# Six instead of seven chunks with a head block taken ahead, two steps sooner, and a tail shared between two engines

## The chip, the cores and the metric

The kernel runs on one NeuronCore of a Trainium2 chip. The core has a matrix engine (PE, with its weight loads as PEld), a vector engine (DVE), a scalar engine (ACT), a general engine (POOL) and a queue engine for DMAs (SP). Each works through its own list of instructions in order; they meet only where one waits for another's result. The metric is the device time of one execution in microseconds (us): the median of the kernel before is 1092.4 us over 3 runs (1090.79 to 1093.73).

## The reference, cut to what matters

Two layers of a transformer on x of shape (16, 256, 128), all in fp32, each with adaptive layer norms: attention and a mixture of 16 experts in the first layer, a "holographic" attention and a channel mix in the second. The change touches only the second layer and how its work is spread over the first layer's experts.

```python
h = _layernorm(x) * (1 + ca) + sa                 # layer 1, first half
k_real = (h @ Wk).reshape(Bb, Tt, H, D)           # H * D = 1024 columns
v = (h @ Wv).reshape(Bb, Tt, H, D)
k = jnp.exp(1j * (k_real * PHASE_SCALE))
rotors = jnp.exp(1j * (t[:, None, None] * freqs))[None]
# _holo_fused_step: real(cumsum(v * binder, over t) * probe) / sqrt(t + 1)
out_pos = _holo_fused_step(v, rotors, jnp.conj(rotors))
k_shifted = jnp.roll(k, 1, axis=1).at[:, 0].set(0.0)
out_assoc = _holo_fused_step(v, jnp.conj(k_shifted), k)
x = x + ga * ((out_pos * g_pos + out_assoc * g_assoc) @ Wo)
h = _layernorm(x) * (1 + cb) + sb                 # layer 1, second half
xr = mu_r * h + (1 - mu_r) * h_prev               # h_prev: h one time step back
xk = mu_k * h + (1 - mu_k) * h_prev
x = x + gb * sigmoid(xr @ W_r.T) * (square(relu(xk @ W_k.T)) @ W_v.T)
```

## The kernel before

The 16 batches are worked on in 8 chunks (`NCH`) of two batches. Tokens lie 128 to a partition block; transposed activations are `128 x 512` tiles (128 channels by two batches of 256 time steps). The program has three stages that follow one another, and a tail.

**Attention** (layer 0) goes over the 64 rounds of batches and heads.

**Experts** (from line 743): one step `n` per chunk `c` and expert `e`, so 128 steps, and 4 more to drain. A step projects gate and up on PE (L764, L766), forms `g` on DVE (L768), `u` on ACT (L770) and Silu on ACT (L773), clips `u` on POOL (L774), multiplies on DVE (L780) and on POOL by the routing weight (L781), and three steps later PE adds the down projection to `acc` (L789). At `e` 2 to 4 of the next chunk the finished chunk goes back into `x`; at `e == 5` DVE takes the figures (means and variances) of the next layer norm and at `e == 7` POOL turns them into a scale and an offset (`normalizer`). PE, DVE, ACT and POOL follow the program's order by hand (`manual_schedule`).

Beside the experts the layer-1 holographic work starts early. Its 1024 columns are 8 blocks of 128 (`NJ`). For the chunks below `AHEAD` (7 of 8) the last block, `j = 7`, is done during the experts of the chunk after, by the generator `part_ahead` (L885). One segment of it runs in each step: `tokens` (layer norm on ACT, L200), two steps later the transposes (L212) and the modulation (L218), then `v` (L899), then the phases `k` (L927), their offset (L944) and sine and cosine (L945 to L950), and then eight pieces (position and association, two batches, sine and cosine). A piece is a product on POOL (`bind`, L905), a running sum on DVE (L911), a product on DVE (L913) and a sum into `total` on DVE (L918). It starts at `e == 10`. For the last of the seven (`soon`, chunk 6, in the experts of chunk 7, which are the last) everything is drawn together: figures at `e == 4`, normalizer at `e == 5`, start at `e == 6`, transposes one step after the tokens, and its pieces are read in six steps. The part of chunk 5 still runs at that time, so two parts end with the experts.

**Holographic stage** (from line 1127): one step `n` per chunk and block, `PARTS[c]` blocks for a chunk: 7 for chunks 0 to 6 and 8 for chunk 7, 57 steps in all. A step is, on PE: keys and values of step `n + 2` (L1158, L1162) and the output projections (L1209, four 512-column matmuls, each seen as two instructions); on DVE: two running sums of 1024 columns (L1195), the phase offset (L1174) and one product (L1426); on POOL: two products for step `n + 1` (L1192) and one for step `n - 1` (L1431); on ACT: two copies out of PSUM (L1159, L1163) and three activations (L1180 to L1182). At block 3 of a chunk with a part ahead, one matmul adds `totals[c]` times `w_last` (L1218). For a chunk from `AHEAD` on, `tokens`, transposes and modulation happen in the chunk before it (L1470, L1475, L1409).

The channel mix of the chunk before runs beside it in places counted from that chunk's end (`place`): output at 0, into `x` at 1, means 2, variances 3, spread 4, norm 5, tokens 6, `pk2` and its squares 7, `pr2` 8, sigmoid and values 9, products 10 and 11, results 12 and 13. What is left for chunk 6 after place 7, and all of chunk 7, is the tail: `last_half` is a generator of six segments, one per batch of chunk 7, and the loop at L1494 goes through both halves segment by segment with the rest of chunk 6 in between. All layer-norm and gating products of both halves are on ACT there (L1358, L1364, L1384).

Tiles of the last stage lie in memory that the expert stage gives back, so their first writers wait for the last readers of what lay there.

## Time and profile before

| what | us | where it is from |
|---|---|---|
| median of the runs (3) | 1092.4 | times |
| the profiled execution's own time | 1093.5 | times |
| its span, first to last instruction | 1091.7 | page |
| attention | 0 to 303.6 | first L764 at 303.6 in the trace |
| experts | 303.6 to 689.4 | ACT takes the last `acc` (L798) at 689.44 |
| of these, experts of chunks 3 and 4 | 45.9 and 45.5 | L764 starts |
| of these, chunk 7 | 631.03 to 689.4 | L764 starts; L798 |
| first product of the next stage on DVE (L1426) | 692.83 | timeline |
| steady chunk of the holographic stage (7 steps) | 46.9 | L1426 starts |
| its last PE result read by ACT (L1227) | 1073.57 | timeline |
| tail, to the last result in `x` | 1088.4 | timeline |
| end of the span (last DMA) | 1091.7 | page |

The time around the span (1093.5 - 1091.7 = 1.8 us) is not changed by anything here. An engine row in a timeline reads: start, duration, engine, line, operation, output<-input, shape, count, and in brackets how long the engine stood idle before it and whose result ended that. Busy times in the page are sums of durations; consecutive instructions on one engine overlap a little, so the distance from one start to the next (0.33 us for a 128x256 DVE instruction whose row says 0.42) is what counts in a dense row.

### The profile page before, as it was taken

The page shows a single profiled execution, that of the slowest core. Times are in us where ns is not written, and L with a number is a line of the kernel's source. Part 1 is how long each engine was busy: PE and PEld are TensorE (multiplying, and loading weights), DVE is VectorE, ACT ScalarE, POOL GpSimd, SP SyncE. Part 2 cuts the span into 40 slices and gives each one's busy share as a digit, 9 for nine tenths or more (in the row PEclk, how much of TensorE's full clock was granted, in tenths as well). Part 3 has the DMA queues.
Part 4 walks back from the last instruction along what each step waited for, and adds up shares of the span by engine and source line. Part 5 has one row for each costly group of instructions (what it writes and reads, how often), then busy time and mean ns, then how long its engine had stood idle before and what let it go on. Part 6 is the DMA issues. An engine that isn't in the chain of part 4 may idle for free.

```text
span 1091.7 us, 16048 instructions
## 1 busy us (share of the span) xinstructions
PE 1025.6 (94%) x5319; PEld 519.0 (48%) x5319; DVE 910.8 (83%) x1417; ACT 687.6 (63%) x1391; POOL 803.1 (74%) x762
## 2 busy tenths in 40 slices
PE   7999999999999999999999999698999999999987
PEld 5566766666654444444444444233344443434333
DVE  6679878998766888887776778998999999999994
ACT  3676766667656476677756555364766766667573
POOL 2245334542658678788876988799999999999992
PEclk8999999999999999999999999799999999999999
DMA  4102100000042222222322221000000000000000
GB/s 115 42 10 69 52 4 3 2 4 3 22 174 82 94 90 86 96 98 78 98 93 81 84 92 58 1 0 0 1 0 10 5 6 10 1 10 1 10 6 24
DMA packets 31955, 46.80 MB, mean 43 GB/s; under 512 B 8032, under 2 KB 22784, under 8 KB 31872
## 3 DMA queue, kind: packets, MB, share of 16 engines
q1 hardware_dynamic: 31328, 45.51, 13.0%
q8 instruction: 42, 0.69, 0.3%
q14 instruction: 41, 0.34, 0.1%
q10 hardware_dynamic: 544, 0.26, 0.1%
HBM read 43.13 MB, written 2.37 MB: 42 GB/s over the span
## 4 chain that ended last, share of the span: by engine, by line
PE 55%; DVE 23%; ACT 8%; POOL 7%; issue 5%; DMA 1%; SPq 0%; DVEq 0%; ACTq 0%; POOLq 0%
PE pg L764 7%; PE acc L789 7%; PE pup L766 7%; DVE mem L1195 6%; DVE sum_assoc L1195 5%; PE s L404 5%; PE st L438 5%; PE po L458 5%; PE pout L1209 5%; DVE m_pos L1426 3%; POOL u L781 2%; PE pq L531 2%; DVE maxima L416 1%; PE pk L1158 1%; PE pk L539 1%
## 5 line engine op out<-in xcount | busy, mean ns | idle before, releaser
L446 ACT ACTIVATE exp<-st 128x512 f32<-128x512 f32 x256 | 132.2, 602 | 87.1 <-PE st L438 87.1
L416 DVE TENSOR_REDUCE maxima<-s 128x2 f32<-128x512 f32 x256 | 158.9, 684 | 26.6 <-PE s L404 26.4
L781 POOL TENSOR_TENSOR u<-u,wide 128x512 f32<-128x512 f32 x128 | 164.0, 1281 | 19.3 <-DVE u L780 10.1
L770 ACT ACTIVATE u<-pup,b_gu 128x512 f32<-128x512 f32 x128 | 87.5, 684 | 102.4 <-PE pup L766 86.4
L768 DVE TENSOR_SCALAR g<-pg,b_gu 128x512 f32<-128x512 f32 x128 | 95.6, 747 | 64.0 <-PE pg L764 63.2
L1209 PE MATMUL pout<-m_pos,w_pos 128*128 128x512 f32 x228 | 115.6, 631 | 31.2 <-DVE m_pos L1426 21.6
L789 PE MATMUL acc<-u,w_dn 128*128 128x512 f32 x256 | 134.3, 606 | 5.9 <-POOL u L781 5.8
L764 PE MATMUL pg<-hT,w_gu 128*128 128x512 f32 x256 | 132.0, 597 | 1.4 <-DVE u L780 0.9
L1195 DVE TENSOR_TENSOR_SCAN sum_assoc<-keep,bound_assoc 128x1024 f32<-128x1024 bf16 x57 | 130.0, 2280 | 1.2 <-POOL bound_assoc L1192 1.2
L766 PE MATMUL pup<-hT,w_gu 128*128 128x512 f32 x256 | 130.7, 592 | 0.0
L1195 DVE TENSOR_TENSOR_SCAN mem<-keep,bound_pos 128x1024 f32<-128x1024 bf16 x57 | 129.6, 2273 | 0.0
L1192 POOL TENSOR_TENSOR bound_assoc<-v,phasor 128x1024 f32<-128x1024 f32 x56 | 122.2, 2183 | 4.8 <-ACT phasor L1182 4.8
L1431 POOL TENSOR_TENSOR sum_assoc<-sum_assoc,phasor 128x1024 f32<-128x1024 f32 x57 | 124.5, 2185 | 0.7 <-DVE sum_assoc L1195 0.7
L1192 POOL TENSOR_TENSOR bound_pos<-v,rotor 128x1024 f32<-128x1024 f32 x56 | 122.3, 2185 | 2.8 <-DVE sums L911 2.8
L774 POOL TENSOR_SCALAR u<-u 128x512 f32<-128x512 f32 x128 | 81.0, 633 | 58.4 <-ACT u L770 51.8
L1209 PE MATMUL pout<-sum_assoc,w_assoc 128*128 128x512 f32 x228 | 107.3, 593 | 0.0
L780 DVE SCALAR_TENSOR_TENSOR u<-u,pg 128x512 f32<-128x512 f32 x128 | 86.9, 679 | 16.9 <-POOL u L774 12.7
L773 ACT ACTIVATE pg<-g 128x512 f32<-128x512 f32 x128 | 76.2, 595 | 27.5 <-DVE g L768 27.2
L1209 PEld LDWEIGHTS pout<-m_pos,w_pos 128*128 128x128 f32 x228 | 40.9, 194 | 101.4 <-DVE m_pos L1426 50.8
L1159 ACT ACTIVATE whole<-pk 128x512 f32<-128x512 f32 x55 | 32.8, 596 | 88.4 <-PE pk L1158 86.0
L438 PE MATMUL st<-qx,kx 32*128 32x256 f32 x1024 | 82.3, 389 | 1.1 <-DMA qx<-turned 1.0
L404 PE MATMUL s<-kx,qx 32*128 32x256 f32 x1024 | 78.2, 409 | 4.2 <-DVE kx L541 1.8
(301 smaller groups left out, 1850.6 us busy)
## 6 DMA issues: line engine op xcount, KB each, us to landing
wide<-scores SPq DMA_DIRECT2D x64, 512.0 KB
qx<-turned SPq DMA_DIRECT2D x256, 1.0 KB
w_gu<-in_gate_up_dram SPq DMA_DIRECT2D x8, 256.0 KB
out_dram<-x SPq DMA_DIRECT2D x16, 128.0 KB
x<-in_x_dram SPq DMA_DIRECT2D x14, 128.0 KB
w_dn<-in_down_dram SPq DMA_DIRECT2D x4, 256.0 KB
ga<-ga_rows SPq DMA_DIRECT2D x1, 768.0 KB
w_k<-in_Wk_dram SPq DMA_DIRECT2D x1, 512.0 KB
```

The lines of the kernel that those rows point to most:

```text
L404: nc.tensor.matmul(s[g][:, i, :], qs[c][r][rows_, k, ts(i, P)], ks[c][rows_, r // NS, k, :], start=True, stop=True,)
L416: nc.vector.tensor_reduce(mx[:, :, g], s[g], AX.X, ALU.max, negate=True)
L438: nc.tensor.matmul(st[g][:, i, :], ks[c][rows_, r // NS, k, ts(i, P)], qs[c][r][rows_, k, :], start=True, stop=True,)
L446: nc.scalar.activation(e[:, g, :, :], st[g], AF.Exp, scale=QSCALE)
L764: nc.tensor.matmul(pg, w_gu[:, e, 0 : 2 * D : 2], h2, start=True, stop=True)
L766: nc.tensor.matmul(pu, w_gu[:, e, 1 : 2 * D : 2], h2, start=True, stop=True)
L781: nc.gpsimd.tensor_tensor(u, u, wide[n // SOME][:, n % SOME, :], ALU.mult)
L789: nc.tensor.matmul(accs[c], w_dn[:, e, :], work.pop(n), start=False, stop=(e == NE - 1))
L1192: nc.gpsimd.tensor_tensor(w[nm], v2, bind, ALU.mult)
L1195: nc.vector.tensor_tensor_scan(dst.rearrange("p s k t -> p (s k t)"), keep.rearrange("p s t -> p (s t)"), work[n][nm].rearrange("p s k t - ...
L1209: nc.tensor.matmul(pos[c], w[:, j, :], m[:, k, :, :].rearrange("p k t -> p (k t)"), start=(j == 0 and i == 0 and k == 0), stop=(j == PARTS ...
L1431: nc.gpsimd.tensor_tensor(m, m, phasor[(n - 1) % 3][:, :, :, 1:], ALU.mult)
```

## The change

`AHEAD` goes from 7 to 6. So chunk 6 keeps all 8 blocks in the holographic stage (58 steps instead of 57), its part ahead with the compressed order (`soon`) is gone, and its tokens, transposes and modulation move into chunk 5's holographic steps. The six parts that remain start at `e == 8` instead of 10.

```diff
-AHEAD = NCH - 1
+AHEAD = NCH - 2
...
-                soon = c == AHEAD - 1
                 tokens(c)
                 yield
-                if not soon:
-                    yield
+                yield
...
-                if soon:
-                    for binds, reads in (((3,), (1,)), ((4,), (2,)), ((5,), (3,)), ((6,), (4,)), ((7,), (5,)), ((), (6, 7))):
-                        go(binds, reads)
-                        yield
-                    return
...
-                    if i and c < AHEAD - 2:
+                    if i:
                         added(pieces[i - 1][1])
...
-                if e == (4 if soon else 5) and c:
+                if e == 5 and c:
                     mv = figures(c - 1, "a1")
-                if e == (5 if soon else 7) and c:
+                if e == 7 and c:
                     figs[c - 1] = normalizer(c - 1, mv, fp, "a1")
...
-                if e == (6 if soon else 10) and 1 <= c <= AHEAD:
+                if e == 8 and 1 <= c <= AHEAD:
                     ahead.append(part_ahead(c - 1))
```

The last output projections go batch by batch, and `pk2` with its squares for chunk 6 leaves the last step for the tail:

```diff
-                out_project(n - 1, 1, w_assoc, m)
-                if n == last + 1:
-                    out_project(last, 0, w_pos, m_pos)
-            if 7 in place:
+                if n <= last:
+                    out_project(n - 1, 1, w_assoc, m)
+                else:
+                    for k in range(2):
+                        for i, (w, read) in enumerate(((w_assoc, m), (w_pos, m_pos))):
+                            for half in range(2):
+                                nc.tensor.matmul(
+                                    pos[NCH - 1][:, ts(k, T)],
+                                    w[:, NJ - 1, :],
+                                    read[:, half, k, :],
+                                    start=False,
+                                    stop=(k == 1 and i == 1 and half == 1),
+                                )
...
+            if 7 in place and n < last:
                 mixed(place[7], wk_now, wk_before, "pk2")
```

In the tail, `last_half` has seven segments. The four POOL instructions for scale and offset become two on DVE (add the epsilon; offset by one `scalar_tensor_tensor`) and one on POOL (the power). The norm of half 0 stays on ACT and that of half 1 goes to DVE; the modulation goes the other way round. The sigmoid's last step goes from ACT to DVE (`tensor_scalar`, add 1, times the gate), for both halves and for chunk 6.

```diff
+            nc.vector.tensor_scalar(rstd, mv[:, :, 1], EPS, None, ALU.add)
+            nc.gpsimd.tensor_tensor(rstd, rstd, neg_half, ALU.pow)
...
+            nc.vector.scalar_tensor_tensor(off, mv[:, :, 0], -1.0, rstd, ALU.mult, ALU.mult)
...
+                if k:
+                    nc.vector.tensor_scalar(
+                        hn[:, i, :], x[b][:, i, :], rstd[:, i : i + 1], off[:, i : i + 1], ALU.mult, ALU.add
+                    )
+                else:
+                    nc.scalar.activation(
+                        hn[:, i, :], x[b][:, i, :], AF.Identity, bias=off[:, i : i + 1], scale=rstd[:, i : i + 1]
+                    )
...
+            if k:
+                nc.scalar.activation(hz[:, 1:], tokens_, AF.Identity, bias=shift, scale=scale)
+            else:
+                nc.vector.tensor_scalar(hz[:, 1:], tokens_, scale, shift, ALU.mult, ALU.add)
...
-            nc.scalar.activation(r, r, AF.Identity, bias=gbT1[:, b : b + 1], scale=gbT1[:, b : b + 1])
+            nc.vector.tensor_scalar(r, r, 1.0, gbT1[:, b : b + 1], ALU.add, ALU.mult)
...
+        both_halves()
+        mixed(gone, wk_now, wk_before, "pk2")
+        mix_squares(gone)
+        mixed(gone, wr_now, wr_before, "pr2", left[:, 0])
+        r = hp.tile([P, 2, T], F32, tag="r", name=f"r_{gone}")
+        nc.scalar.activation(r, mix[gone], AF.Tanh, scale=0.5)
+        mix[gone, "r"] = r
+        mix_values(gone, left[:, 1])
+        both_halves()
+        both_halves()
+        for k in range(2):
+            nc.vector.tensor_scalar(r[:, k, :], r[:, k, :], 1.0, gbT1[:, 2 * gone + k : 2 * gone + k + 1], ALU.add, ALU.mult)
+            mix_gated(gone, k)
+        both_halves()
+        py = with_tokens_first(gone, mix.pop((gone, "r")), "py2", (p_out, "out"))
+        both_halves()
+        for k in range(2):
+            mix_out(2 * gone + k, py[:, k])
+        both_halves()
+        both_halves()
```

## The prediction

> **What bounds the kernel now.** I read the page's chain first, then busy time by stretches, then the timelines of the stretches where a bound changes hands.
>
> ```profile
> PE 55%; DVE 23%; ACT 8%; POOL 7%; issue 5%; DMA 1%; SPq 0%; DVEq 0%; ACTq 0%; POOLq 0%
> 631.00:664.00 33.00, 32.10 (x79) 14.16 (x78) 23.73 (x47) 18.71 (x35) 27.45 (x35) 1.00 0.28 96
> 664.00:694.00 30.00, 20.33 (x43) 7.79 (x41) 29.09 (x52) 10.85 (x19) 21.07 (x28) 0.88 0.05 18
> 694.00:1073.60 379.60, 347.76 (x838) 149.42 (x838) 362.20 (x280) 241.07 (x512) 369.05 (x185) 0.99 0.02 5
> ```
>
> The columns after a stretch are its length and the busy time of PE, PEld, DVE, ACT and POOL, then the granted clock. The experts are PE's (32.1 of 33.0), but their last 30 us are not: DVE is busy for 29.1 and PE for 20.3. Later POOL (97%) and DVE (95%) are both full. The timelines of that gap, PE, POOL and DVE:
>
> ```profile
> 654.21 1.49 PE L212 MATMUL pln_a<-ident,hn_a 128*128 128x128 f32 x4 [0.72 <-ACT hn_a L200]
> 676.38 1.13 PE L764 MATMUL pg<-hT,w_gu 128*128 128x512 f32 x2 [0.94 <-DVE u L780]
> 685.14 1.12 PE L789 MATMUL acc<-u,w_dn 128*128 128x512 f32 x2 [1.73 <-POOL u L781]
> 687.33 2.08 PE L789 MATMUL acc<-u,w_dn 128*128 128x512 f32 x2 [1.06 <-POOL u L781]
> ...
> 692.48 2.17 POOL L1192 TENSOR_TENSOR bound_pos<-v,rotor 128x1024 f32<-128x1024 f32 x1 [2.78 <-DVE sums L911]
> 694.61 2.17 POOL L1192 TENSOR_TENSOR bound_assoc<-v,phasor 128x1024 f32<-128x1024 f32 x1
> 696.75 2.18 POOL L1431 TENSOR_TENSOR sum_assoc<-sum_assoc,phasor 128x1024 f32<-128x1024 f32 x1
> ...
> 690.64 0.49 DVE L913 SCALAR_TENSOR_TENSOR sums<-sums,gates,phasor_ahead 128x256 f32<-128x256 f32 x1
> 691.17 0.42 DVE L918 TENSOR_TENSOR total<-sums,total 128x256 f32<-128x256 f32 x1
> 691.70 0.70 DVE L911 TENSOR_TENSOR_SCAN sums<-sums,und_ahead_assoc 128x256 f32<-128x256 f32 x1
> ```
>
> PE's last gate projection starts at 676.38 and its last `acc` only at 687.33. DVE is still summing pieces of the parts ahead at 691.70, and POOL's first product of the next stage waits 2.78 us for exactly that. From 692.48 POOL runs without a gap, 2.13 us from start to start, and the chain of waits goes through it to 736. So the next stage's clock starts at POOL's 692.48.
>
> **Part 1, the hand-over: -14.1 us.** Without the part of chunk 6, the stretch before 694 loses eight pieces on DVE: sum, product and addition, from start to start 0.73 + 0.53 + 0.34 = 1.60, so 12.8, and one offset (L944, 0.68). 29.1 busy of 30 becomes about 16: DVE no longer holds anything. PE loses `v` and `k` (two matmuls of 0.86), the transposes (0.44) and waits. Chunk 7's steps, from the L764 starts, were 2.57, but 4.26 at `e` = 3, 4.78 at 7, 3.44 and 3.43 at 8 and 9, and 3.68 at 14; without them 2.21 + 0.87 + 0.86 + 1.11 = 5.05 go, and the last gate projection starts at 676.38 - 5.05 = 671.33. What follows it I take from a quiet step, 522.53 in chunk 4: `g` ends 1.8 later, ACT's `u` and Silu at 3.2, POOL's clip at 3.6, DVE's product at 4.4, POOL's product at 5.7, and PE's `acc` needs 0.9 more: 678.0, where ACT could take `acc` only at 689.44 (half the clock then: 0.88 on average over the stretch). POOL's two small memsets (they waited for PE's `acc` in the trace too) take 0.3, so POOL starts at about 678.4 instead of 692.48: -14.1. The remaining part, of chunk 5, ends its last sum in step 127, before DVE's last expert product, so the 2.78 us wait has nothing left to wait for. DVE's first running sum then starts at about 676 and the second is done by 682; POOL needs it at 678.4 + 2 x 2.13 = 682.7. Bounds: -16, and -7.9 if the drain stays as long as it was (rival 1).
>
> **Part 2, two steps sooner: -1.5 us.** The parts of chunks 1 to 4 find steady PE-bound steps, and the same instructions merely change places: `v` and `k` at `e` 11 and 12 instead of 13 and 14. New is that `tokens` now follow `normalizer` by one step. In chunk 4 POOL ends its normalizer at 515.96 and ACT would be free for the tokens at 515.4: ACT waits 0.6 and is through at 517.65, its next `u` (516.78) comes 0.9 late, but POOL's clip of it started only at 518.70 and PE reads the tokens two steps later, at 520. Cost nothing; the cover is POOL's queue, and rival 2 is what it costs without it. One collision goes. In chunk 2's step `e` = 3 (6.73 us against 4.26 in chunk 3) ACT runs the router's exponential between the sines of part 0:
>
> ```profile
> 398.25 1.28 ACT L283 ACT_TABLE_LOAD   x1
> ...
> 400.04 1.28 ACT L950 ACT_TABLE_LOAD   x1
> ...
> 402.64 1.28 ACT L773 ACT_TABLE_LOAD   x1
> ```
>
> Two steps sooner the sine (L950) is before the exponential, and one of three loads goes (1.28). I take -1.5 with a little of the half clock that followed (407.2 to 410.6 at 0.50); bounds -3 and +2, the latter if the tokens at `e` = 8 of chunk 1 delay a DVE that is full with routing there.
>
> **Part 3, one step more: +6.75 us.** A step on the dense stretch takes POOL 3 x 2.13 = 6.40 and DVE 2.20 + 2.19 + 0.60 + 1.13 = 6.1. The L1426 starts give 6.10 to 6.43 for plain steps and 7.12, 7.30, 6.78 for the first three of a chunk. The work after chunk 6 spreads over one step more: `pk2` (1.72 on PE) falls in step 7 of chunk 6, `pr2` in the first of chunk 7. I put 7.0, 7.0, 7.3, three times 6.43, 5.96, 6.05 = 52.6 where the last chunk had 46.07: +6.5. Moving chunk 6's tokens and modulation into chunk 5 costs what chunk 7's cost in chunk 6, 6.68 instead of 6.43 in one step: +0.25. The dropped `w_last` matmul (0.86 on PE) is hidden. Bounds 6.1 and 7.6.
>
> **Part 4, the tail: -1.0 us.** Without `pk2` in the last step, PE's last projections start when POOL's product is ready (1069.25 instead of 1069.93) but then wait for DVE's (1070.5): they end 0.3 sooner. From there, counted from ACT's first `oT` (1073.57), before:
>
> ```profile
> 1076.66 0.60 ACT L1309 ACTIVATE r<-left 128x512 f32<-128x512 f32 x1 [2.25 <-PE left L1258]
> 1077.29 1.09 ACT L1312 ACTIVATE r<-r,gbT 128x256 f32<-128x256 f32 x2
> 1078.28 0.86 ACT L1358 ACTIVATE hn_last<-x,off_last,rstd_last 128x128 f32<-128x128 f32 x2
> ...
> 1080.51 0.87 ACT L1358 ACTIVATE hn_last<-x,off_last,rstd_last 128x128 f32<-128x128 f32 x2
> ```
>
> and the last result at 1088.43, 14.86 after. Now PE does `pk2` and `pr2` of chunk 6 first (1.72 each, 1.17 to 4.6); ACT's squares and tanh end at 5.25, so half 0's norm on ACT ends at 6.1 (5.6 before), while half 1's on DVE is ready at about 5.6 (7.8 before). Transposes to 6.6; modulation on DVE to 6.9, on ACT to 7.2 (8.8 before). Then PE in order: two `pk` 0.86 each to 8.6, chunk 6's transposes to 9.05, two `pr` to 10.75; tanh 11.2, DVE's scaling 11.55, chunk 6's two results 12.2, two products 12.95, transposes 13.2, last result 13.9: -0.95. I give 0.25 back for four output DMAs where two were. A DVE `tensor_scalar` of 128x256 in SBUF is not in the trace; I price it at 0.33 to 0.42 like other 128x256 rows (L1323), the tiny ones at 0.06 (a 128x4 memset) to 0.28 (reciprocal of 128x20), taking 0.2. Bounds of the part: -2.5 and +1.0.
>
> The Trainium skill, "VectorE: DVE Perf Modes", section "Mode 2×_2P", lets an fp32 `tensor_scalar` with source and result in SBUF run two elements a cycle; L849 (128x512 in SBUF, 0.77 us) shows no such halving. By the page the four scalings would save some 0.15 each, an estimate of 0.6 and a tail of -1.6.
>
> **Sum.** -14.1 - 1.5 + 6.75 - 1.0 = -9.85 on the span, 1091.7 to 1081.85. The profiled execution's own time is 1093.5, its surroundings stay at 1.8, so 1083.65 for that execution; against the median of 1092.4, which lies 1.1 below it, **1082.5**. About 0.3% (3.3 us) is what a measurement of this kernel can tell from no change.
>
> **Rivals.** 1, *the drain stays long*. The part of chunk 5 still sums until step 127, and if it or memory handed over holds DVE and POOL as now, the 13 us from last gate projection to finished `acc` (676.38 to 689.4) remain and the hand-over gives 5.05 + 2.8 = 7.9: 1082.5 + 6.2 = 1088.7. For it: ACT waits 2.28 there for nothing that the profile shows. Against it: DVE's load halves.
>
> 2, *the tokens stall PE in each of six chunks*, the slower side. Where the tokens follow one step after the normalizer today, in chunk 7, ACT waited 1.9 for POOL and PE stood (the L212 row). With a half-clock piece after it such a stall cost 2.47 in chunk 2. Six of them, 14.8, give 1097.3; from 1.64 a chunk the whole gain is gone. Against it: PE now reads the tokens two steps later.
>
> 3, *the half clock of 745.1 to 748.5 goes as well*. There PE waited 3.74 for `oT`; the distance between L1426 starts is 9.10, against 7.30 in later chunks. The pause is 3.74 long and may miss the window that decides: -1.8, 1080.7. Beside it, the Trainium skill ("TensorE: Matmul & The Clock Gate", "What's actually happening") has the clock set by free-running windows of about 3.4 us; the 3.4 us pieces agree.
>
> 4, *the parts cancel*: the step costs 7.6, the tail +1.0, and rival 1 holds: -7.9 - 1.5 + 7.6 + 1.0 = -0.8, 1091.6.
>
> **Chances.** Forecast 0.68, own range 1078.5 to 1087; rival 1 0.13, rival 2 0.06, rival 3 0.08, rival 4 0.05. Faster takes the forecast, rival 3 and two thirds of rival 1: 0.85; the rest of rival 1 and rival 4: 0.09; slower 0.06. Range 1077.5 to 1089.5: it leaves out rivals 2 and 4 and the ends of the others.
>
> **What would show it.** Part 1: POOL's first L1192 within 7 to 8 us of the last L764, no wait on L911. Part 2: two table loads around L283, chunk 2 at 46 to 47, no idle PE before L212. Part 3: 52 to 53 us from the L1426 start of chunk 6's eighth step to the last one. Part 4: last result 13 to 14.5 after `oT`. Wrong would be a late POOL start, or expert chunks over 46.5 throughout.

## The result, and the profile after

The changed kernel takes 1081.49 us, the median of 6 runs (1079.34 to 1084.76), beside 1091.79 us for the kernel before in 6 runs of the same chip. The ratio is 0.9905, with a 95% interval of 0.9892 to 0.9919: about 1% faster, 10.3 us. The profiled execution took 1081.84 us with a span of 1080.1 us.

First the page's chain of waits, by engine, and then busy time by stretches of the kernel after: length, then the busy time of PE, PEld, DVE, ACT and POOL with their instructions, then the granted clock, the share of the DMA engines and GB/s.

```profile
PE 59%; DVE 23%; ACT 6%; POOL 6%; issue 4%; DMA 1%; SPq 0%; DVEq 0%; ACTq 0%; POOLq 0%
```

```profile
628.00:658.00 30.00, 30.00 (x73) 13.25 (x72) 23.63 (x47) 13.73 (x25) 26.43 (x34) 1.00 0.26 92
658.00:676.00 18.00, 16.74 (x39) 7.11 (x38) 15.32 (x25) 7.03 (x13) 15.29 (x20) 1.00 0.14 53
676.00:1061.90 385.90, 351.75 (x860) 151.50 (x858) 368.90 (x283) 247.33 (x525) 376.70 (x188) 0.99 0.02 5
```

The last chunk of the experts is PE's throughout: 30.0 of 30, and 16.7 of the last 18, drain included. Before, PE had 20.3 of the last 30. The share of PE in the chain rises from 55% to 59%, that of ACT and POOL falls. In the long stage POOL stays full (376.7 of 385.9) and DVE nearly so (368.9); it is one step longer.

Now the hand-over of the kernel after, as timelines of PE, POOL and DVE. In this kernel the lines have moved: L1172 are the running sums (before L1195), L1169 the two products on POOL (L1192), L1413 the third (L1431), L1408 DVE's product (L1426), L1186 the output projections (L1209), L1204 `oT` (L1227); of a piece, L903 is the product, L909 the sum, L911 the product and L916 the addition.

```profile
668.50 1.02 PE L764 MATMUL pg<-hT,w_gu 128*128 128x512 f32 x2
673.26 2.35 PE L789 MATMUL acc<-u,w_dn 128*128 128x512 f32 x4 [1.17 <-POOL u L781]
...
671.94 2.49 POOL L781 TENSOR_TENSOR u<-u,wide 128x512 f32<-128x512 f32 x2
675.73 0.10 POOL L1021 MEMSET phasor<- 128x4 f32 x1 [1.30 <-PE acc L789]
675.86 2.18 POOL L1169 TENSOR_TENSOR bound_pos<-v,rotor 128x1024 f32<-128x1024 f32 x1
...
670.82 0.42 DVE L916 TENSOR_TENSOR total<-sums,total 128x256 f32<-128x256 f32 x1
673.42 2.30 DVE L1172 TENSOR_TENSOR_SCAN mem<-keep,bound_pos 128x1024 f32<-128x1024 bf16 x1
```

From the last gate projection to POOL's first product of the next stage it is 675.86 - 668.50 = 7.36 us (7.37 from the unrounded times), where it was 16.1. No sum of a part ahead stands there any more: the last addition starts at 670.82, and what POOL waits for is PE's `acc`.

The same points in both traces divide the gain. "S" is the start of POOL's first product of the next stage.

| us | before | after | difference | forecast |
|---|---|---|---|---|
| first gate projection of the experts | 303.62 | 303.41 | -0.2 | - |
| chunk 2 of the experts | 48.50 | 46.54 | -1.96 | -1.5 for chunk 2 and all |
| chunk 6 of the experts | 48.10 | 47.31 | -0.79 | 0 |
| the other chunks up to chunk 7's first projection | | | -0.1 | 0 |
| chunk 7's first projection to its last | 45.36 | 40.50 | -4.86 | -5.05 |
| drain, last projection to S | 16.09 | 7.37 | -8.72 | -9.05 |
| S to the last product on DVE (L1426, now L1408) | 376.78 | 381.82 | +5.04 | +6.75 |
| from there to ACT's first `oT` | 4.31 | 4.18 | -0.13 | -0.3 |
| `oT` to the end of the span | 18.15 | 18.20 | +0.05 | -0.7 |

They add up to -11.7, the difference of the two spans within rounding (1091.7 - 1080.1 = 11.6). One more thing matters below: the start of the experts itself varies from 300.9 to 303.6 us between the profiled executions, in kernels that are equal up to there, so experiments are compared by **the span less the first gate projection**, 788.1 before and 776.7 after, beside their medians.

### The profile page after: what moved, and what is told of

Same layout as the page of the kernel before. It is cut to its first block, busy times and chain, and to the rows that moved or that the text cites. A ratio compares the mean times of both kernels' runs of the same rounds, so it can differ in the third digit from the quotient of the medians.

```text
span 1080.1 us, 16033 instructions
## 1 busy us (share of the span) xinstructions
PE 1023.5 (95%) x5333; PEld 519.6 (48%) x5333; DVE 909.9 (84%) x1409; ACT 682.3 (63%) x1383; POOL 803.1 (74%) x750
## 4 chain that ended last, share of the span: by engine, by line
PE 59%; DVE 23%; ACT 6%; POOL 6%; issue 4%; DMA 1%; SPq 0%; DVEq 0%; ACTq 0%; POOLq 0%
PE pg L764 9%; PE acc L789 9%; PE pup L766 9%; DVE sum_assoc L1172 7%; DVE mem L1172 6%; PE s L404 5%; PE st L438 5%; PE po L458 5%; DVE m_pos L1408 4%; PE pout L1186 3%; PE pq L531 2%; DVE maxima L416 1%; POOL bound_pos L1169 1%; POOL u L781 1%; PE pk L539 1%
## 5 line engine op out<-in xcount | busy, mean ns | idle before, releaser
L781 POOL TENSOR_TENSOR u<-u,wide 128x512 f32<-128x512 f32 x128 | 163.9, 1281 | 16.1 <-DVE u L780 6.3
L1186 PE MATMUL pout<-m_pos,w_pos 128*128 128x512 f32 x228 | 114.7, 627 | 32.1 <-DVE m_pos L1408 23.2
L768 DVE TENSOR_SCALAR g<-pg,b_gu 128x512 f32<-128x512 f32 x128 | 95.6, 747 | 58.2 <-PE pg L764 56.9
L1172 DVE TENSOR_TENSOR_SCAN sum_assoc<-keep,bound_assoc 128x1024 f32<-128x1024 bf16 x58 | 132.3, 2282 | 1.8 <-POOL bound_assoc L1169 1.7
L1172 DVE TENSOR_TENSOR_SCAN mem<-keep,bound_pos 128x1024 f32<-128x1024 bf16 x58 | 131.9, 2274 | 0.0
L1169 POOL TENSOR_TENSOR bound_assoc<-v,phasor 128x1024 f32<-128x1024 f32 x57 | 124.3, 2181 | 3.9 <-ACT phasor L1159 3.9
L1413 POOL TENSOR_TENSOR sum_assoc<-sum_assoc,phasor 128x1024 f32<-128x1024 f32 x58 | 126.6, 2183 | 0.4 <-DVE sum_assoc L1172 0.4
L1169 POOL TENSOR_TENSOR bound_pos<-v,rotor 128x1024 f32<-128x1024 f32 x57 | 124.4, 2182 | 0.0
L1186 PE MATMUL pout<-sum_assoc,w_assoc 128*128 128x512 f32 x228 | 107.5, 594 | 1.2 <-POOL sum_assoc L1413 1.2
L1186 PEld LDWEIGHTS pout<-m_pos,w_pos 128*128 128x128 f32 x228 | 40.4, 192 | 102.0 <-DVE m_pos L1408 53.5
L773 ACT ACTIVATE pg<-g 128x512 f32<-128x512 f32 x128 | 76.1, 594 | 16.8 <-DVE g L768 16.7
```

The lines of the kernel that those rows point to most:

```text
L781: nc.gpsimd.tensor_tensor(u, u, wide[n // SOME][:, n % SOME, :], ALU.mult)
L1169: nc.gpsimd.tensor_tensor(w[nm], v2, bind, ALU.mult)
L1172: nc.vector.tensor_tensor_scan(dst.rearrange("p s k t -> p (s k t)"), keep.rearrange("p s t -> p (s t)"), work[n][nm].rearrange("p s k t - ...
L1186: nc.tensor.matmul(pos[c], w[:, j, :], m[:, k, :, :].rearrange("p k t -> p (k t)"), start=(j == 0 and i == 0 and k == 0), stop=(c < NCH - ...
L1413: nc.gpsimd.tensor_tensor(m, m, phasor[(n - 1) % 3][:, :, :, 1:], ALU.mult)
```

## The experiments

Twelve kernels were run, each beside the kernel before on the same chip.

**No pieces.** The kernel before; in the part of chunk 6 the eight pieces are left out and its `total` is set to 0, so chunk 6's last block is missing from what this kernel computes.

```diff
             def part_ahead(c):
...
+                if soon:
+                    nc.vector.memset(totals[c], 0.0)
...
                 def go(binds, reads):
+                    if soon:
+                        return
```

> The kernel before, with chunk 6's part ahead reduced to its tokens, v, phases and sines; its eight products, sums and additions (POOL and DVE) are left out and its total is set to 0, so chunk 6's last block is missing from the result. Theory (the hand-over was held by the vector engine's pieces): from the last gate projection to POOL's first product of the next stage 16.1 us become 7.4 as in the changed kernel, and the 1.1 us stall before the last projection goes: about -9.8 us, 1082. Rival (the drain is long by itself or by memory handed over): the 16.1 us stay at 13 or more and the time at 1088 or above.

Measured: median 1084.15, ratio 0.9922 (0.9903 to 0.9941), 778.5 after the first projection, 9.6 less than before. The drain was 7.65, so these pieces are nearly all of what the drain lost (8.4 of 8.7). Chunk 7's projections took 44.25, only 1.1 of the 4.9 less: the other 3.75 are left for the tokens, transposes, `v` and `k`, which this kernel keeps.

**Which engine's half of the pieces.** Two more kernels split them: one leaves out only the sums, products and additions on DVE (its `total` is 0 as well), the other only the products on POOL, so that DVE's sums read `v` itself in their place.

```diff
-                    for q in reads:
+                    for q in reads if not soon else ():
```

```diff
                 def bind(nm, k, s, by):
+                    if soon:
+                        bound[nm, k, s] = v[:, k, :]
+                        return
```

> The kernel before with POOL's eight products of the scores' last part kept and the sums, products and additions on VectorE that follow them left out (that part's total is set to nought). Theory: VectorE holds the hand-over, so the drain from the last gate product to POOL's first product of the next stage falls to 7.4 to 8 us as it did with all of it left out, span less start near 778.5 to 779, median near 1084 us. Rival: POOL's own eight products (0.7 us each, 5.6 us) hold it, so the drain stays at 12 us or more and the median near 1088 us.

> The kernel before with POOL's eight products of the scores' last part left out and the sums, products and additions on VectorE kept (they read the values themselves in the products' place). With both kinds the drain from the last gate product to POOL's first product of the next stage was 16.09 us, with POOL's alone 12.14, with neither 7.65. Theory: the two engines share the blame, each waiting for the other, so VectorE's reads alone leave a drain near 11.6 us (16.09 less the 4.5 that POOL's products alone cost), median near 1087.5 us. Rival: VectorE is full by itself (29.1 of 30 us) and holds the drain at 14.5 us or more, median 1090 us or more; POOL's products then only fill the room that VectorE leaves.

| part of chunk 6, kernel before | drain, us | median, us | ratio (95%) |
|---|---|---|---|
| all of it | 16.09 | - | - |
| without POOL's products | 16.02 | 1091.34 | 0.9998 (0.9988 to 1.0007) |
| without DVE's work | 12.14 | 1087.77 | 0.9963 (0.9949 to 0.9976) |
| without both | 7.65 | 1084.15 | 0.9922 (0.9903 to 0.9941) |

Both of my theories fell here. The first said that DVE alone held the hand-over; with its work gone the drain was still 12.1. The second, made after that, said that the two shared the blame; with POOL's products gone nothing changed. What the four rows show is two ceilings, one above the other. DVE is the higher one: with its work kept, POOL's makes no difference. Under it lies POOL. Its timeline without DVE's work:

```profile
675.75 0.61 POOL L774 TENSOR_SCALAR u<-u 128x512 f32<-128x512 f32 x1
676.44 1.26 POOL L781 TENSOR_TENSOR u<-u,wide 128x512 f32<-128x512 f32 x1
677.66 0.72 POOL L905 TENSOR_TENSOR bound_ahead_pos<-v_ahead,rotor 128x256 f32<-128x256 f32 x1
678.35 0.63 POOL L905 TENSOR_TENSOR und_ahead_assoc<-v_ahead,phasor_ahead 128x256 f32<-128x256 f32 x1
679.06 0.61 POOL L774 TENSOR_SCALAR u<-u 128x512 f32<-128x512 f32 x1
```

There is not one wait in brackets: clip, routing product and two pieces take 3.31 us a step (675.75 to 679.06), where PE needs 2.57. POOL's list is not quite all of the 4.5 us that this kernel's drain is longer than the one without both: after its last product `u` POOL waits 2.25 for PE's last `acc`, where it waits 1.30 there; the granted clock was 0.50 from 678.2 to 685.1. And the timeline of DVE and POOL without POOL's products:

```profile
688.91 0.70 DVE L914 TENSOR_TENSOR_SCAN sums<-sums,v_ahead 128x256 f32<-128x256 f32 x1
689.65 0.49 DVE L916 SCALAR_TENSOR_TENSOR sums<-sums,gates,phasor_ahead 128x256 f32<-128x256 f32 x1
...
689.69 2.17 POOL L1195 TENSOR_TENSOR bound_pos<-v,rotor 128x1024 f32<-128x1024 f32 x1 [2.71 <-DVE sums L914]
```

POOL waits 2.71 us for DVE's last sum (L914 in that kernel), as it waited 2.78 for it before. No result of that sum goes into POOL's product; the sum is one of the last readers of memory that the next stage writes over, so I read this as a wait for memory; no run here tests that by itself.

**Two steps sooner, alone.** The kernel before; the first six parts start at `e == 8`, the seventh is left as it was.

```diff
-                if e == (6 if soon else 10) and 1 <= c <= AHEAD:
+                if e == (6 if soon else 8) and 1 <= c <= AHEAD:
```

> The kernel before, with the first six parts started at e = 8 instead of 10 and the seventh as it was. Theory: chunk 2 loses one table load and about 2.0 us, chunk 6 about 0.8, and chunk 5's last piece ends two steps sooner, which frees up to 1.6 us at the hand-over: 1087.4 to 1089. Rival (tokens one step behind the normalizer stall PE): every expert chunk 1.6 us or more longer, 1097.

Measured: median 1087.63, ratio 0.9958 (0.9943 to 0.9973), and 784.1 after the first projection, 4.0 less than before. Chunk 2 takes 46.54 and chunk 6 47.31, just as in the kernel after, and the drain goes to 14.30, which is 1.8 of the 4.0. Rival 2, a stall in each chunk, is refuted: no chunk became longer.

**Two steps later in the changed kernel.**

```diff
-                if e == 8 and 1 <= c <= AHEAD:
+                if e == 10 and 1 <= c <= AHEAD:
```

> The changed kernel with its six parts started at e = 10. Theory: the exponential of the router stands between two sines again (three table loads), chunk 2 is back at 48.5 us and chunk 6 0.8 longer: 2.8 us slower than the changed kernel, about 1084.3. The hand-over stays short, since the last piece (1.6 us on DVE) ends in the time in which POOL still finishes the experts. Rival (the two steps sooner are what frees the hand-over): POOL's first product of the next stage waits for a sum of a piece again and the kernel is 5 us or more slower than the changed one.

Measured: median 1083.31, ratio 0.9918 (0.9904 to 0.9933), 779.8 after the first projection, 3.1 more than after. Chunk 2 is back at 48.49, chunk 6 at 48.08, and the drain is 7.73. Put in or taken out, the earlier start is worth 3 to 4 us in the traces, twice what I gave it. The medians alone would not say so here: the ratio is 0.9918 against 0.9905 after, 1.4 us, with overlapping intervals. What carries the reading is that chunks 2 and 6 repeat within 0.05 us in every kernel with the same start and the same parts.

**The old tail in the changed kernel.** All edits of the last step and the tail are undone (last projections, `last_half`, the order after it).

```diff
-        def both_halves():
+        for part in range(6):
             for half in halves:
                 next(half)
...
-                if k:
-                    nc.vector.tensor_scalar(
-                        hn[:, i, :], x[b][:, i, :], rstd[:, i : i + 1], off[:, i : i + 1], ALU.mult, ALU.add
-                    )
-                else:
-                    nc.scalar.activation(
-                        hn[:, i, :], x[b][:, i, :], AF.Identity, bias=off[:, i : i + 1], scale=rstd[:, i : i + 1]
-                    )
+                nc.scalar.activation(
+                    hn[:, i, :], x[b][:, i, :], AF.Identity, bias=off[:, i : i + 1], scale=rstd[:, i : i + 1]
+                )
```

> The changed kernel with the old tail and the old order of the last projections. Theory from the two traces (first oT to end of span 18.24 us after, 18.13 before; last L1426 product to oT 4.18 and 4.31): the tail's part of the change gave nothing, so the time stays within 0.5 us of the changed kernel. Rival (the prediction's part 4): 1.0 us slower than the changed kernel.

Measured: median 1083.02, ratio 0.9918 (0.9901 to 0.9935), its interval overlapping that of the kernel after (0.9892 to 0.9919); 776.9 after the first projection, 0.2 more than after. From `oT` to the last result it takes 14.87 us, as before the change, and 14.75 with the new tail. The new tail is worth next to nothing in the traces; the runs alone cannot tell it from the 1.0 us of the forecast. The one piece of it that came as forecast is the order of the last projections: from the last product on DVE to `oT` it takes 4.51 here and 4.18 in the kernel after, 0.3 less.

**A part less still.**

```diff
-AHEAD = NCH - 2
+AHEAD = NCH - 3
```

> The changed kernel with parts ahead for five chunks only: chunk 5 keeps its eighth block too (59 steps). Theory (only the part that ended with the experts was dear, because it kept DVE busy past them; the others are covered by PE's own time): one more holographic step, 5.1 to 6.1 us, against v, k and the transposes that leave PE in chunk 6 (0.86 + 0.86 + 0.44 = 2.2), the drain stays at 7.4: 3 to 4 us slower than the changed kernel. Rival (a part ahead costs the experts more than its step costs later): the gain goes on, 3 us or more faster than the changed kernel.

Measured: median 1085.32, ratio 0.9947 (0.9932 to 0.9962), 782.0 after the first projection, 5.3 more than after. S to the last product grew by 5.4, chunk 6 of the experts fell by only 0.6 (2.2 expected) and chunk 7 grew by 0.4, and the drain stayed at 7.37. So the sixth part ahead costs the experts 0.2 us in all and saves 5.4 later, where the seventh cost more than it saved. The five parts before these were not tried one by one.

**The order of `oT` and the cosines.** The chain of waits of the kernel after, at the first step of a chunk (start, length, what):

```profile
1012.58 0.64 ACT phasor L1157
1013.21 0.02 issue
1013.24 0.64 ACT off L1158
1013.88 0.02 issue
1013.90 0.72 ACT phasor L1159
1014.62 0.73 ACT oT L1204 x2
1015.36 0.04 issue
1015.40 1.98 PE pout L1186 x4
```

ACT computes the sine and cosine of the step after next (L1157 to L1159, 1012.58 to 1014.62), and only then copies out the finished chunk's `oT`, which PE's next projection waits for. In chunk 1 PE waits longest. Two kernels put `oT` ahead of the cosines, the first for chunk 1 only, the second for every chunk:

```diff
+            early_gate = j == 0 and 1 <= c < NCH
+            if early_gate:
+                o = gated_out(c - 1)
...
-            if j == 0 and c:
+            if j == 0 and c and not early_gate:
```

> The changed kernel with the scaling of chunk 0's projected output (ACT, oT) put ahead of the cosines in the first step of chunk 1. Theory (the half clock after it and the 8.81 us step come from PE's 3.84 us wait for oT): PE waits 2.1 us, for DVE's product, the half clock at 728 does not come, the step falls to 6.1 to 6.5: about 2.5 us faster than the changed kernel. Rival (the half clock comes in any case): the step stays above 8 us, the time within 0.7 us.

> The changed kernel with oT ahead of the cosines in the first step of every chunk. Theory (the 7.12 us of a chunk's first step are the wait for oT behind the cosines, not the channel mix's matmuls): these steps fall to 6.1 to 6.4; POOL's own 6.40 us a step and 1.25 a chunk allow at most 0.87 us a chunk: 2.5 + 6 x 0.7 = 6.7 us faster than the changed kernel. Rival (the cosines, 0.8 us later, then hold POOL and DVE): no faster than the kernel with this in chunk 1 alone.

For chunk 1: median 1079.92, ratio 0.9897 (0.9882 to 0.9911), 776.2 after the first projection, 0.4 less than after, where 2.5 were expected. The first step of chunk 1 fell from 8.81 to 6.40, and the half clock near 728 us is gone; but a later step (`n` = 12) rose from 6.10 to 7.64, so most of it was given back. PE's row in the kernel after, and with the order changed:

```profile
727.86 3.68 PE L1186 MATMUL pout<-m_pos,w_pos 128*128 128x512 f32 x4 [3.84 <-ACT oT L1204]
```

```profile
724.47 1.96 PE L1186 MATMUL pout<-m_pos,w_pos 128*128 128x512 f32 x4 [2.20 <-DVE m_pos L1408]
```

The same four matmuls take 3.68 us behind a wait of 3.84, and 1.96 behind one of 2.20.

For every chunk: median 1076.07, ratio 0.9862 (0.9847 to 0.9876), 772.7 after the first projection, 4.0 less than after, where 6.7 were expected. First steps of a chunk take 6.38 to 6.42 in place of 7.12, but one later step of a chunk takes 6.9. The local cause is shown; what the whole gains is read from POOL. First its one wait in chunk 6 of the kernel after, then two small instructions of the channel mix's norm in the kernel with `oT` ahead:

```profile
977.78 2.18 POOL L1169 TENSOR_TENSOR bound_assoc<-v,phasor 128x1024 f32<-128x1024 f32 x1 [1.05 <-ACT phasor L1159]
```

```profile
980.66 1.02 POOL L1266 TENSOR_TENSOR rstd_f<-off_f,neg_half 128x4 f32<-128x4 f32 x1
981.77 0.20 POOL L1267 TENSOR_TENSOR less_f<-less_f,rstd_f 128x4 f32<-128x4 f32 x1
```

A step takes POOL 6.40 (three products, 2.13 each from start to start), and once a chunk the two small instructions take 1.26 more (the next product starts at 981.92), 46.1 for seven steps. With `oT` ahead in every chunk, a chunk takes just that (46.1, from 46.9), so the later 6.9 is no new loss. From S to the last product on DVE, POOL's waits of over 0.15 us add up to 4.3 us in the kernel after and to 0.3 with `oT` ahead, and the stretch is 4.1 shorter. In the kernel after they stand in chunks 2 to 6, one in each, and one at the end. In chunk 1 none stands, so the 2.4 us of its long first step were not there to be won.

**The order in the tail.** Rows of ACT, PE and DVE in the kernel after:

```profile
1066.66 0.60 ACT L1497 ACTIVATE r<-left 128x512 f32<-128x512 f32 x1 [0.46 <-PE left L1235]
1067.15 0.87 ACT L1339 ACTIVATE hn_last<-x,off_last,rstd_last 128x128 f32<-128x128 f32 x2
...
1067.31 1.12 PE L1295 MATMUL left<-ka,w_v 128*128 128x512 f32 x2 [0.69 <-ACT r L1497]
1068.27 0.60 PE L1345 MATMUL pln_last<-ident,hn_last 128*128 128x128 f32 x4
...
1073.91 0.35 DVE L1365 TENSOR_SCALAR r_last<-r_last,gbT 128x256 f32<-128x256 f32 x1 [0.51 <-ACT r_last L1364]
1074.18 0.75 DVE L1303 TENSOR_TENSOR x<-py,x 128x256 f32<-128x256 f32 x2
1074.84 0.75 DVE L1369 TENSOR_TENSOR r_last<-pv_last,r_last 128x256 f32<-128x256 f32 x2
1075.85 0.76 DVE L1303 TENSOR_TENSOR x<-py_last,x 128x256 f32<-128x256 f32 x2 [0.26 <-PE py_last L1373]
```

Two things stand in the way. Chunk 6's value matmul (L1295) waits for its tanh (L1497) and stands ahead of the transposes (L1345) on PE, and half 0's norm on ACT (L1339) stands behind the same tanh: the transposes come at 1068.27. And DVE does chunk 6's results (L1303) ahead of the last products (L1369), which the end waits for. The first kernel below takes only the second away; the other both, and puts chunk 6's value matmul behind the transposes (the second cut shows what it has besides the first).

```diff
         py = with_tokens_first(gone, mix.pop((gone, "r")), "py2", (p_out, "out"))
-        both_halves()
         for k in range(2):
             mix_out(2 * gone + k, py[:, k])
         both_halves()
+        both_halves()
         both_halves()
```

```diff
         mixed(gone, wr_now, wr_before, "pr2", left[:, 0])
+        both_halves()
         r = hp.tile([P, 2, T], F32, tag="r", name=f"r_{gone}")
         nc.scalar.activation(r, mix[gone], AF.Tanh, scale=0.5)
         mix[gone, "r"] = r
-        mix_values(gone, left[:, 1])
-        both_halves()
         both_halves()
+        mix_values(gone, left[:, 1])
```

> The kernel after with only chunk 6's two results in the tail moved ahead of the last gates. Theory: the results of chunk 6 cost the tail the 0.66 us that they take ahead of the last two products, so oT to last result falls from 14.75 to near 14.1 us and the rest of the 1.35 us comes from the norm ahead of the tanh. Rival: the wait for r_last takes it up and 14.7 us stays; the norm's place is all of it.

> The changed kernel with another order in the tail: half 0's norm ahead of chunk 6's tanh on ACT, chunk 6's value matmul behind the transposes of the norms on PE, and chunk 6's two results on DVE ahead of the last halves' gates instead of behind them. Theory (the tail's gain was lost to order: the two results, 0.66 us, stand ahead of the last products on a DVE that had idled 2.4 us before; the transposes waited for a norm behind the tanh): last result 13.7 to 13.9 us after oT instead of 14.75, 0.9 us faster than the changed kernel. Rival (PE's order of the last matmuls sets the end): within 0.3 us.

Measured from `oT` to the last result: 14.75 after, 14.09 with the results moved, 13.40 with both. Medians 1080.25, ratio 0.9893 (0.9880 to 0.9907), and 1078.49, ratio 0.9881 (0.9865 to 0.9898); after the first projection 775.9 and 775.3. So 0.66 came from the results and 0.69 from the norm and the value matmul. The rows with both:

```profile
1064.49 0.88 ACT L1339 ACTIVATE hn_last<-x,off_last,rstd_last 128x128 f32<-128x128 f32 x2
1065.27 0.57 ACT L1498 ACTIVATE r<-left 128x512 f32<-128x512 f32 x1
...
1069.45 0.76 DVE L1303 TENSOR_TENSOR x<-py,x 128x256 f32<-128x256 f32 x2 [1.02 <-PE py L1212]
1071.87 0.75 DVE L1369 TENSOR_TENSOR r_last<-pv_last,r_last 128x256 f32<-128x256 f32 x2
```

The norm now starts as soon as ACT's squares are done, and chunk 6's results fall into a stretch in which DVE is idle.

**Both orders.** The edits of the kernel with `oT` ahead in every chunk and of the tail with both moves.

> The kernel after with both orders: the oT product ahead of the cosines in the first step of every chunk, and in the tail the norm of half 0 ahead of chunk 6's tanh with chunk 6's results ahead of the last gates. Theory: they lie in different stages and add: hand-over to last m_pos near 377.7 us, oT to last result near 13.4 us, median near 1074.7 us (1.4 below the kernel with the first order alone). Rival: the end of the holographic loop shifts by the order and the tail's gain is already in it: at most 0.5 us below that kernel.

Measured: median 1075.32 of 5 runs (1073.97 to 1077.92), ratio 0.9847 (0.9832 to 0.9861). S to the last product takes 377.5 and `oT` to the last result 13.39, so in the trace both gains stand, and 771.0 after the first projection is 1.7 under the kernel with `oT` ahead alone. The intervals of these two overlap, so by the runs alone the 1.6 us between the ratios (0.0015 of 1092) is likely, not certain. Of the kernels run here it has the lowest time: 16.5 us under the one before and about 6 under the change as made.

## Why the prediction was right, and where it was not

The forecast of 1082.5 us lies 1.0 above the median of 1081.5. The direction, the mechanism and the largest term were right. That it is so close is in part luck: on the two spans -9.85 was forecast and -11.6 measured, and the misses of the four parts, +0.5, -1.3, -1.7 and +0.9 (minus is a larger gain), partly cancel.

**Part 1, the hand-over.** Forecast -14.1, measured -4.86 - 8.72 = -13.6. The two components fit one by one (5.05 and 9.05). Leaving out the pieces alone gave the same drain. What the prediction did not have is POOL as a second ceiling: it said that DVE holds the hand-over, which is right, but by its reading taking away DVE's work would have been enough, and that would have given 4 of the 8.4 us. The sum came out because the change takes the part from both engines at once. Rival 1, the drain that stays long, fell: its condition, that one remaining part is enough to hold DVE or POOL, did not hold.

**Part 2, two steps sooner.** Forecast -1.5, measured -2.8 (1.96 in chunk 2, 0.79 in chunk 6, 0.1 in the others). The mechanism was right. ACT's timeline of the kernel after:

```profile
395.11 0.71 ACT L936 ACTIVATE phasor_ahead<-size_ahead,half_pi 128x512 f32<-128x512 f32 x1
...
398.59 1.28 ACT L283 ACT_TABLE_LOAD   x1
401.11 0.47 ACT L283 ACTIVATE rt_exp<-rt_exp 128x320 f32<-128x320 f32 x1 [1.23 <-DVE rt_exp L282]
...
402.17 1.28 ACT L773 ACT_TABLE_LOAD   x1
```

The sine (L936) is done before the first load, and two loads are left of three. The 3.4 us of half clock near 405 to 407 stand in every kernel here whose parts start at `e == 10` and in none with `e == 8`, and chunk 2 fell by 1.96. The size was off in two ways. In chunk 2 more goes than the load (1.28) and the 0.2 that I gave to the half clock: steps `e` 3 and 4 fall from 9.83 to 6.98, nearly the whole stall, while steps 0 and 1 rise from 5.14 to 6.04, which the prediction did not have. And I put the effect on chunk 6 at nothing, where 0.79 went. The two experiments with `e` at 8 and 10 moved both chunks by the same amounts. In chunk 6 of the kernel before, PE's `acc` waits 0.27 for POOL's `u` (at 620.18), and in the kernel after no wait stands in these steps; the rest of the 0.79 stays open.

**Part 3, one step more.** Forecast +6.75, measured +5.04. From the product of chunk 6's eighth step to the last it took 51.38 us (forecast 52.6; the last seven steps before took 46.07). The step that failed is the 7.0 for chunk 6's eighth step, in which a `pk2` falls: it took 6.10. PE in the kernel after, in that step, and DVE's products at its two ends:

```profile
1006.39 1.02 PE L1234 MATMUL pk<-shifted,wk_now 128*128 128x512 f32 x2
1007.25 1.02 PE L1235 MATMUL pk<-shifted,wk_before 128*128 128x512 f32 x2
1008.11 1.88 PE L1186 MATMUL pout<-m_pos,w_pos 128*128 128x512 f32 x4
...
1006.30 1.21 DVE L1408 TENSOR_TENSOR m_pos<-mem,rotor 128x1024 f32<-128x1024 f32 x1
1012.40 1.21 DVE L1408 TENSOR_TENSOR m_pos<-mem,rotor 128x1024 f32<-128x1024 f32 x1
```

The 1.72 us of `pk2` fit into the time that PE has over. I had put the long first steps of a chunk down to such work of PE's; the experiment with `oT` ahead shows that 0.7 of the 7.12 is `oT` behind the cosines, and that belongs to a change of chunk, of which there are as many as before. The forecast of 52.6 was too long by 1.2, 0.9 of it here. The tokens of chunk 6 cost nothing, since they moved from one step to another: 6.43 to 6.68 in chunk 5, and 6.68 to 6.43 in chunk 6. I had counted the first alone, 0.25. The last 0.2 lie in the steps of the stage's start. POOL's list gives the same sum from the other side: a step more is 6.40 on it, its waits of over 0.15 us from S on fall from 5.55 to 4.31 in all (one of 1.03 in chunk 7 is gone), and 6.40 - 1.24 = 5.2.

**Part 4, the tail.** Forecast -1.0, measured about -0.1; undoing it moved the time by less than the runs can tell. The last result, at 14.75 after `oT`, lies outside the 13 to 14.5 that the prediction named. The step that failed is "transposes to 6.6". Half 0's norm ended 6.2 us after `oT` (1067.15 + 0.87 - 1061.86), close to my 6.1, and half 1's a little sooner; but I had left chunk 6's value matmul out of PE's list. It stands ahead of the transposes, waits for the tanh and holds PE from 1067.31 to 1068.27, so the transposes end at 7.0 (1068.27 + 0.60). PE's `pk` starts 7.4 after `oT`, where my working had 6.9, and from there everything is late by 0.5 to 0.85: the last result comes at 14.75, not 13.9. With both orders changed it comes at 13.40, under the working: the gain was in the edit and was lost to the order of two queues. The tiny instructions on DVE were sized right (0.15 to 0.17 where I took 0.2).

The rule of the Trainium skill, "VectorE: DVE Perf Modes", section "Mode 2×_2P", was put aside with a row of 0.77 us. That row was a mean over four, and the single ones say otherwise. DVE's L849 in the kernel after, then POOL at the first of them:

```profile
340.48 1.47 DVE L849 TENSOR_SCALAR rotor<-theta 128x512 f32<-128x512 f32 x1
431.07 0.42 DVE L849 TENSOR_SCALAR rotor<-theta 128x512 f32<-128x512 f32 x1
```

```profile
340.39 1.27 POOL L781 TENSOR_TENSOR u<-u,wide 128x512 f32<-128x512 f32 x1
```

Three of the four `tensor_scalar` of 512 elements in SBUF take 0.42 here, what a two-input instruction takes for 256 (L1300), so the trace agrees with the doubled rate. In the kernel before they took 0.49, 0.63, 0.49 and, the first, 1.47. With its input in PSUM, one of 128x512 takes 0.75 (L768). The 1.47 stands under a product of POOL's that starts 0.09 before it and ends at 341.66, though neither waits for the other's result. The Trainium skill, "GPSIMD Engine Reference", section "1. Specifications", says that POOL's interfaces to SBUF are shared with DVE and that the two contend when DVE uses both its ports or takes two inputs from SBUF. This row fits that; no run here tests it. The four scalings of 128x256 in the tail took 0.34 to 0.35, 0.07 to 0.08 less than a two-input instruction of that shape, about half of the 0.15 estimated from the page.

**Rival 3,** the half clock, did not come: the wait for `oT` grew from 3.74 to 3.84 and the half clock stood at 728.0 to 731.4. The experiment on chunk 1 made it go away, but the kernel gained 0.4 and not the 1.8 of the rival, since POOL had no wait there. **Rival 2** fell with the start at `e == 8`. **Rival 4** needs rival 1, a step of 7.6 and a tail of +1.0, and none of the three came.

## What to carry to other kernels

Work hidden in another stage can be nearly free while that stage's bound has steady work to run beside it, and dear at its end: the last of seven parts ahead cost 13.6 us of hand-over and saved 5.0, the sixth saves 5.4 and costs the experts 0.2. Before saying that an engine holds a stretch, ask what the next engine's list would take if the first were free; here one engine's work gone brought 4 us, the other's alone nothing, both 8.4. Before pricing a long step, look whether the engine that bounds the stage waits in it: the step of 8.81 us in chunk 1 gave 0.4, because POOL had work through all of it, and the chunks in which POOL waited gave the rest. And a shared tail is won by its queues' order, not by the number of engines: the same instructions gave 0.1 us in one order and 1.35 more in another.

## What the runs showed of the hardware

- The half clock at the start of the program, near 20 us, lasted 3.4 us in some profiled executions and 6.8 in others, and the experts started at 300.9 to 301.8 or at 302.6 to 303.6 accordingly, in kernels equal up to that point: a spread of some 2 us, as large as some of the effects looked for here. Counting from the first projection takes it out.
- The length of one wait of PE does not decide whether the clock halves. In the kernel after, a wait of 3.84 us was followed by 3.41 us at half the clock (from 728.01), and so was a wait of 2.28 (from 687.05); with `oT` ahead in chunk 1, a wait of 2.20 (up to 724.47) was not. The pieces begin on a grid: 687.05 and 728.01 lie 12 x 3.41 us apart, and in the kernel before 407.18, 687.08, 704.14 and 745.10 lie 82, 5 and 12 such lengths apart. So it matters how a wait falls on the grid. Two windows of it ahead of a fall in the kernel after, then the one with most of the 2.20:

```profile
683.64:687.05 3.41, 1.13 (x3) 0.30 (x2) 3.37 (x4) 1.45 (x3) 3.41 (x3) 1.00 0.00 0
724.60:728.01 3.41, 0.15 (x1) 0.15 (x2) 3.20 (x3) 2.71 (x5) 3.41 (x2) 1.00 0.00 0
```

```profile
723.14:726.55 3.41, 2.08 (x5) 1.06 (x6) 3.20 (x3) 1.99 (x4) 3.41 (x2) 1.00 0.00 0
```

  PE was busy for 1.13 and 0.15 us ahead of a fall, and for 2.08 where none came. No single bound comes out of the traces, though: in the kernel before the clock fell at 407.2 after a window in which PE was busy for 2.17 us (403.79 to 407.20). Beside these rows, the Trainium skill, "TensorE: Matmul & The Clock Gate", section "What's actually happening", lets the clock fall after an idle window of about 3.4 us. The length of the pieces agrees; but the windows ahead of these falls were not idle throughout, and there the measurement decides.
- A change of ACT's table took 1.28 us, and the next instruction ran 0.02 us behind it (398.25 + 1.28, then the exponential at 399.55 in the kernel before).
